# Two sequences' dispatch gathers as one step in the same four PSUM banks, in two of four sublayers of a two-layer macaron network

## The chip, the cores and the metric

The kernel runs on one core of a Trainium2 chip. A core has five engines with a queue each: TensorE (PE; its weight loads are listed as PEld) multiplies matrices into PSUM, VectorE (DVE) and ScalarE (ACT) read PSUM and SBUF, GpSimd (POOL) works in SBUF, and SyncE (SP) issues all DMA transfers here. The metric is device time in microseconds (us). The kernel before takes 718.74 us (median of three runs, 718.47 to 719.14).

## The reference, cut to what matters

The input is eight sequences of 256 tokens with 128 features, in float32.

```python
x = x + 0.5 * soft_moe(layernorm(x))       # 16 experts x 64 slots
x = x + linear_attention(layernorm(x))     # 16 heads, elu + 1
x = x + 0.5 * soft_moe(layernorm(x))
x = x + 0.5 * ternary_glu(layernorm(x))
x = x + favor_attention(layernorm(x))      # 16 heads, 32 random features
x = x + 0.5 * ternary_glu(layernorm(x))
# soft_moe, the part that the change touches (x normalized once more, se the slots' keys):
logits   = einsum('bnd,esd->bnes', x, se)          # 256 tokens x 1024 slots per sequence
dispatch = softmax(logits, axis=1)                 # over the tokens
combine  = softmax(logits over all slots)
slots    = einsum('bnd,bnes->besd', x, dispatch)   # "the gather": 1024 slots x 128 features
eout     = (gelu(slots @ Wg + bg) * (slots @ Wu + bu)) @ Wd + bd     # per expert
out      = einsum('bns,bso->bno', combine, eout)
```

## The kernel before, in words

The sequences are worked in two groups of four (G, BG). Both soft_moe sublayers of a group share one routine, so there are four such sublayers: (group 0, layer 0), (0, 1), (1, 0) and (1, 1). Between them run `linear` (after layer 0) and, after layer 1, `glu`, `favor` and `glu` again. The group's sublayer does `dispatch` for each of its four sequences, then `experts` once for the four together, then `combine` for each.

`dispatch(b)` normalizes the tokens, transposes them on TensorE (L455), and sends them out to DRAM and back (`replicated`, L637 to L652) so that a "k4" tile `yr` holds each 32-token block on its own quarter of the partitions. The logits (L670) are made with slots on partitions, 1024 slots as eight blocks of 128, and copied into a "comb" tile, from which the combine weights come later. A second "comb" tile `ex` takes the exponentials (L709), which GpSimd divides by their sums (L722) and VectorE transposes in blocks of 32 x 32 (L730), so that tokens stand on partitions. The gather (L743) then uses TensorE split into four groups of 32 rows: each group a multiplies its 32-token block with `ex` into a PSUM bank of its own, 256 columns wide, accumulating over the eight blocks c. Each PSUM bank holds 512 float32 values a partition; the gather fills half of each of four banks. Four evacuations (`affinely`, L557: ScalarE at L560 or VectorE at L562) scale and shift the banks into the "slots" tile `sl`. After that `dispatch` goes on to the maximum over slots (L758 to L790) and the exponentials of the combine weights (L796, L802).

`experts(sl)` fetches each expert's weights, 448 KB, into one of six "we" tiles (L823), multiplies the slots of all four sequences at once (L837), applies gelu on ScalarE (L843) and the product on VectorE (L848), multiplies back (L868), adds the bias (L874), and places the result over the slots by DMA (L881). `combine` (L910) multiplies the combine weights with it. The ternary layers' large products are L1124, their first and last ones L1193, L1196 and L1221; `favor` uses the column split (L1278, L1347, L1382: 32 columns of the array each) and the row split (L1297).

The order of all this is fixed in the file. Every piece of work is a `step`: the engines that may do it with an expected duration, what it reads and writes, and which tiles it takes. `ORDER` lists the steps' numbers; a negative number means the second of the two engines that a step allows (VectorE in place of ScalarE, GpSimd in place of VectorE). `Plan.place` goes through the list, gives each step the earliest time its engine, its inputs and a free tile allow, and picks the tile that has been free longest. It charges TensorE for a change between full array, row split and column split (`SPLIT`, L214) and ScalarE for a change of function table (`TABLE`). `Plan.issue` then writes out the instructions by planned start, each engine's in that order; where TensorE is planned to wait over 700 ns on a bank, it adds dummy matmuls (L1440). The tiles come in pools of fixed size (`kinds`, L327): nine "comb" of 8 KB a partition, four "k4" of 4 KB, eight PSUM banks "ps".

Of the kernel before, what the change touches and what calls it, by code (L numbers as in the profile page):

```python
# [16 lines left out]
    10, 11, 0, 37, 38, 3, 19, 20, 1, 2, 7, 8, 6, 4, 5, 13, 12, 40, 39, 41, 43, 53, 44, 42, 21, 22,  # L17
    23, 24, 14, 132, 133, -136, 172, 62, 63, 31, 134, 136, 137, 15, 16, 17, 18, 142, 140, 60, 9,
    143, 141, 32, 25, 26, -34, -35, 35, 36, 56, 1329, -28, 92, -29, 93, -96, -95, 98, 61, 173,
    1286, 1287, 148, -1290, 149, 29, -31, 68, 138, -1289, 146, 147, 57, 144, -146, 96, 97, 69,  # L20
    150, 66, 67, 64, 65, 163, 1292, 100, 73, -175, 104, 105, 70, 101, 102, 103, 106, 107, 164,
    139, -176, 176, 108, 1290, 177, 182, -1292, 180, 1294, 1330, -1332, -1333, 1333, 165, 166, 71,
    74, 178, 153, 109, 1334, 75, 76, 186, 187, 181, 184, 167, 72, 113, 114, 151, 183, 1345, 77,
    99, 154, 78, 82, 79, 80, 185, 81, 110, 1302, 1339, 51, 1295, 1337, 1338, 83, 115, 1342, 111,
    112, 116, 188, 155, 156, 117, 118, 193, 1335, 1336, 189, 1340, 152, 50, 1341, 190, 191, 194,
    119, 157, -123, 1343, 179, -121, 195, 1344, 1347, 121, 1346, 196, 192, 197, 158, 1299, 1348,
    160, 159, 162, 49, 161, 1349, 168, 48, 355, 203, 198, 200, -202, -200, 1372, 1296, 204, 1415,
    84, 85, 205, 202, 359, 366, 370, 1416, -1419, 1297, 1298, 1301, 1303, 360, 361, 356, 1304,
    357, 358, 1373, -1375, 250, 251, 252, 253, 1375, 1350, 1351, 254, 324, 325, 326, 1300, 328,
    334, 1353, 1376, 1377, 1310, 1305, 367, 379, 86, 368, 87, 88, 369, 206, -1418, 373, 338, 335,  # L30
    374, 219, 255, 256, 268, 90, 329, 371, 330, 372, 376, 327, 269, 1382, -208, 210, 341, 123,
    342, 1388, 339, 340, 336, 337, 1380, 1363, 1306, 1381, 170, 1384, 377, 220, 1307, 124, 125,
    -1390, 52, 345, 1385, 1354, 1355, 261, 223, 352, 353, 221, -1384, 224, 1387, 1378, 1356, 346,
    1386, 1320, 349, 350, 292, 293, 262, 225, 222, 347, 263, 1293, 1390, 1406, 236, 237, 296, 297,
    351, 1352, 265, 266, 281, 348, 264, 294, 1407, 1408, 240, 244, 1308, 241, 295, 242, 1409, 245,
    267, 47, 1357, 303, 298, 246, 304, 305, 306, 362, 363, 307, 308, 270, 1358, 243, 208, 209,
    1396, 310, 1421, 375, 1391, -1361, 378, 1311, 311, 278, 279, 1392, 1393, 1321, 1322, -1411,
    1411, 1312, 354, 257, 258, -1362, 1397, 271, 272, 1364, 273, 309, 274, 1365, 212, 213, 214,
    216, 275, 276, 229, 230, 231, 1398, 215, 233, 282, 1313, 286, 234, 235, 1362, 313, 217, 218,
    283, 317, 323, 1394, 1379, 232, 312, 287, 314, 1359, 364, 288, 238, 284, 277, 1419, 318, 319,  # L40
    285, 315, 316, 280, 1399, 1400, 1395, 259, 344, 1413, 1323, 1324, 169, 320, 321, 1420, 1366,
    343, 289, 290, 226, 227, 228, 91, -1368, 291, 1422, 126, 127, 130, 331, 131, 1309, 1412, 239,
    1370, 247, 1314, 248, 299, 1368, 332, 333, 1325, 260, 211, 1401, 1402, 171, 300, 1369, 249,
    1315, -1319, -1320, 301, 1316, 322, 1612, 1428, 1429, 1431, 1432, 89, 1538, -1404, 1439, 1423,
    1425, -1405, 1440, -1427, 1441, -1318, 365, 302, 1496, 459, 1424, 1434, 1427, 1435, 1436,
    1326, 381, 128, 45, 380, 382, 1442, 129, 1443, 433, 1437, 1528, 1438, 1327, 1430, 383, 384,
    432, 458, 434, 1517, 435, 1433, -386, 460, 461, 386, 1444, 1549, 1446, 436, 1448, 406, -1448,
    387, 1328, 388, -438, 407, 389, -439, 462, 463, 1405, 464, 1445, 1518, 408, 465, 1449, 439,
    1542, 1543, 1616, 1613, 1614, 409, 410, 412, 411, 1544, 1497, 1498, 1500, 1501, 1499, 1519,
    1520, 1539, 1540, 1617, 1521, 1529, 1550, 1551, 1553, 1541, 1615, 442, 1618, 440, 413, 1502,  # L50
    1514, 1530, 1554, 1555, 1552, 1515, 466, 1450, 1451, 1532, 1522, 1523, 441, 443, 445, 1452,
    1531, 391, 1533, 414, 1535, 416, 468, 1453, 1454, 1371, 1536, 467, 446, 1622, 1623, 444, 449,
    448, 469, 470, 1534, 1548, 1458, 474, 1456, 471, 472, 473, 1459, 392, 397, -397, 475, 1556,
    1566, 447, 393, 394, 395, 1507, 1567, 1537, 1511, 1512, 1513, 1508, 1509, 1510, 1460, 1461,
    1465, 1469, 1557, 390, 476, 477, 398, 1470, 1471, 46, 1466, 1467, 450, 415, 399, 417, 451,
    1468, 1601, 1414, 1569, 1591, 478, 400, 401, 1524, 1525, 479, 1545, 1546, 402, 419, 1462, 403,
    404, 405, 418, 422, 1568, 484, 485, 1475, 1516, 480, 420, 421, 1595, 423, 1596, 452, 453,
    1605, 1606, 1482, 1483, -488, 1547, 454, 1479, 1602, 486, 1597, -456, 1463, 1486, 1607, 1490,
    1558, 1464, 1603, -482, 456, 1604, 488, 457, 570, 571, 1487, 1488, 489, 573, 1472, 1473, 1476,
    1477, 482, 1478, 1625, 483, 613, 614, 1580, 1584, 1585, 1491, 54, 55, 1492, 492, 494, -494,  # L60
    496, 1506, -616, 497, -499, 495, 500, 501, -617, 617, 618, 424, 425, 1592, 426, 1581, 1611,
    1480, 1489, 499, -573, 1503, 1481, 1593, 1594, 502, 1582, 1583, 1457, 508, 574, 1608, 621,
    509, 626, 1609, 622, -576, 578, 1455, 427, 623, 503, 1504, 619, 629, 624, 518, 1559, 1563,
    510, -580, 1586, 1570, 1474, 490, 625, 491, 627, 628, 631, 632, 504, 505, 1527, 580, 1610,
    582, 583, 584, 511, 512, 1598, 1624, 1599, 1493, 1494, 1495, 519, 520, 630, 581, 1564, 1560,
    1561, 1562, 428, 1565, 506, 507, 1571, 1572, 429, 1619, 1620, 1485, 1574, 1575, 1576, 1577,
    430, 431, 527, 528, 1505, 1621, 633, 513, 1578, 1573, 1587, 529, 530, 531, 532, 637, 634, 635,
    638, 1484, -516, 1588, 589, 586, 537, -588, 585, 588, 535, 594, 540, 543, -545, 536, 541, 539,
    542, 514, 1579, 636, 1590, 1600, 1526, 1589, 1653, 639, 1652, 640, 521, 620, 576, 577, 1678,
    538, 546, 545, 551, 595, 596, 641, 1679, 597, 590, 591, 592, 552, 1680, 1654, 1655, 1656,  # L70
    -1658, 598, 1627, 553, 1626, 1628, 522, 547, 533, 548, -517, 517, 642, 644, 646, 593, 599,
    -1659, 643, 1659, -646, 549, 550, 554, 561, 555, 600, 534, 556, 559, 1629, 604, 558, 1660,
    -604, 1630, -1632, 1632, 557, 1662, 1705, 1633, 1681, 1682, -1685, 1704, 1706, 562, 563, 602,
    1707, 1708, 673, 799, -1684, 560, 601, 677, 678, 679, 1634, 674, 675, 803, 804, 805, 647, 800,
    810, 778, 782, 1661, -1710, 1710, 1711, 779, 1714, 726, 801, 802, 780, 1685, 676, 811, 812,
    648, 649, 684, 783, 784, 814, 815, 1664, -1669, 1669, 816, 813, 1635, 691, 688, 689, 820, 692,
    1637, 1639, 1638, 1712, 1686, 525, 821, 690, 781, 685, 686, 687, 1663, 1665, 1713, 1642, 1643,
    789, 1715, 1717, 564, -566, 1687, 1640, 1641, 701, 702, 796, 1644, 817, 1645, 1646, 1666,
    1667, 566, 567, 730, 797, 1647, 58, 1689, 1691, 1648, 1649, 1716, 1721, -1721, 818, 568, 1690,
    757, 1695, 1718, 1719, 1670, 1671, 523, 1692, 656, 660, -1695, 657, 1693, 1636, 1722, 1723,  # L80
    1672, 1673, 661, 727, 1724, 1725, 1688, 1650, 728, 729, 736, 1651, 790, 731, 732, 761, 650,
    651, 1696, 662, 1726, 1730, 743, 744, 762, 763, 1727, 663, 667, 791, 693, 1728, 1729, 668,
    669, 605, 1674, 1675, 704, 1731, 1697, -1734, 606, 793, -1733, 1734, 664, 683, 658, -1736,
    1859, 1860, 822, 1676, -1863, 1698, 1677, 1773, 1774, 652, 794, 795, 1699, 1746, 659, 792,
    1747, 1738, 1740, 1739, 1742, 1743, 1745, 665, 806, 705, 709, 1748, 703, 809, 666, 1700, 1701,
    807, 710, 737, 1744, 1754, 819, 607, 1741, 1749, 1702, 1703, 608, -1777, 738, 758, 759, 760,
    -1776, 706, -1862, 1865, 1863, -1865, 707, 740, 739, 680, 711, 681, 1869, 708, 741, 775, 776,
    654, 1867, 1750, 798, 1868, 768, 823, -1871, 1878, 1751, 1777, 569, 1779, 1875, 670, 671,
# [220 lines left out]
def macaron_kernel(ctx: ExitStack, tc: tile.TileContext, i: dict, out: bass.AP):  # L309


    nc = tc.nc
    B, N, D = out.shape
# [1211 lines left out]
```

## Time and profile before

| | |
|---|---|
| median of three runs | 718.74 us |
| the profiled execution | 720.09 us, of which the span from first to last instruction 718.4 us |
| TensorE busy | 710.3 us, 5266 matmul records |
| VectorE, ScalarE, GpSimd busy | 496.6, 391.4, 326.6 us |
| the gather (L743) | 1024 records, 59.5 us busy |
| its evacuations (L560, L562, "slots") | 42 and 22 instructions, 570 and 533 ns |
| granted TensorE clock | 1.00 |

The profile is one execution, recorded by the hardware. Float32 matmuls show as two records each, so 64 records of L743 are one sequence's gather (eight blocks times four row groups). A group's line gives the source line, engine and operation, the tiles written and read, the shapes, the number of instructions, then the engine's busy time, the mean duration, and the idle time just before them with the work that ended it. The chain that ended last is listed in order of time as start, length, engine, tile, line and records. Waits are "who <- released by whom: us in total, times, longest".

### The profile page before, as it was taken

The page shows a single profiled execution, that of the slowest core. Times are in us where ns is not written, and L with a number is a line of the kernel's source. Part 1 is how long each engine was busy: PE and PEld are TensorE (multiplying, and loading weights), DVE is VectorE, ACT ScalarE, POOL GpSimd, SP SyncE. Part 2 cuts the span into 40 slices and gives each one's busy share as a digit, 9 for nine tenths or more (in the row PEclk, how much of TensorE's full clock was granted, in tenths as well). Part 3 has the DMA queues.
Part 4 walks back from the last instruction along what each step waited for, and adds up shares of the span by engine and source line. Part 5 has one row for each costly group of instructions (what it writes and reads, how often), then busy time and mean ns, then how long its engine had stood idle before and what let it go on. Part 6 is the DMA issues. An engine that isn't in the chain of part 4 may idle for free.

```text
span 718.4 us, 14349 instructions
## 1 busy us (share of the span) xinstructions
PE 710.3 (99%) x5266; PEld 609.3 (85%) x5266; DVE 496.6 (69%) x1087; ACT 391.4 (54%) x780; POOL 326.6 (45%) x432
## 2 busy tenths in 40 slices
PE   8999999999999999999999999999999999999998
PEld 6889889998899999999788879876886878868787
DVE  7999774767997688974534545787576877875432
ACT  4987677464865547784642544566435542452421
POOL 6848377531327355745884321352425563413020
PEclk9999999999999999999999999999999999999999
DMA  4553566154344644462642321023404143241001
GB/s 134 162 201 99 165 160 225 34 157 124 118 113 134 182 133 127 120 195 90 203 137 67 84 67 43 18 61 89 73 16 89 44 92 58 59 90 30 12 11 37
DMA packets 118741, 72.76 MB, mean 101 GB/s; under 512 B 73360, under 2 KB 107536, under 8 KB 118672
## 3 DMA queue, kind: packets, MB, share of 16 engines
q1 hardware_dynamic: 118672, 71.85, 36.0%
q8 instruction: 42, 0.69, 0.4%
q14 instruction: 27, 0.22, 0.1%
HBM read 51.89 MB, written 11.53 MB: 88 GB/s over the span
## 4 chain that ended last, share of the span: by engine, by line
PE 95%; POOL 2%; DMA 1%; ACT 1%; DVE 1%; issue 0%; POOLq 0%; ACTq 0%
PE ps L1124 27%; PE ps L837 15%; PE ps L743 8%; PE ps L910 8%; PE ps L868 7%; PE ps L670 7%; PE ps L1221 4%; PE ps L1193 4%; PE ps L1196 4%; PE ps L455 2%; PE ps L1297 1%; PE ps L1347 1%; PE ps L1382 1%; PE ps L958 1%; DMA we<-in_We 1%; POOL sm L486 1%
## 5 line engine op out<-in xcount | busy, mean ns | idle before, releaser
L837 PE MATMUL ps<-slots,we 128*128 128x256 f32 x512 | 122.5, 380 | 1.8 <-ACT k L843 0.9
L837 PEld LDWEIGHTS ps<-slots,we 128*128 128x128 f32 x512 | 92.9, 190 | 14.8 <-ACT slots L560 1.2
L1124 PE MATMUL ps<-comb,comb 128*128 128x256 f32 x448 | 103.0, 380 | 0.0
L1124 PE MATMUL ps<-comb,slots 128*128 128x256 f32 x448 | 102.5, 380 | 0.0
L1124 PEld LDWEIGHTS ps<-comb,slots 128*128 128x128 f32 x448 | 84.1, 190 | 13.2 <-issue 1.8
L1124 PEld LDWEIGHTS ps<-comb,comb 128*128 128x128 f32 x448 | 83.6, 190 | 13.1 <-issue 1.7
L843 ACT ACTIVATE k<-ps,small 128x256 f32<-128x256 f32 x128 | 57.5, 475 | 60.1 <-PE ps L837 52.5
L796 POOL TENSOR_TENSOR comb<-comb,k 128x1024 f32<-128x1024 f32 x32 | 75.4, 2364 | 31.3 <-ACT k L460 8.8
L722 POOL TENSOR_TENSOR comb<-comb,sm 128x1024 f32<-128x1024 f32 x32 | 60.3, 1895 | 41.5 <-DVE sm L717 37.8
L848 DVE SCALAR_TENSOR_TENSOR k<-ps,small,k 128x256 f32<-128x256 f32 x128 | 57.4, 476 | 19.5 <-ACT k L843 18.2
L460 ACT COPY k<-ps 128x512 f32<-128x512 f32 (+2 forms) x52 | 25.6, 497 | 78.9 <-PE ps L1124 56.1
L868 PEld LDWEIGHTS ps<-we,k 128*128 128x128 f32 x512 | 63.6, 192 | 4.8 <-issue 2.0
L709 ACT ACTIVATE comb<-comb,sm 128x256 f32<-128x256 f32 x128 | 63.6, 507 | 4.6 <-DVE sm L701 2.4
L868 PE MATMUL ps<-we,k 128*128 128x128 f32 x512 | 65.7, 276 | 0.0
L484 POOL TENSOR_SCALAR sm<-sm 128x2 f32<-128x2 f32 x52 | 10.0, 193 | 121.7 <-DVE sm L478 112.1
L1138 DVE TENSOR_TENSOR comb<-ps,k 128x512 f32<-128x512 f32 x48 | 32.6, 686 | 47.1 <-PE ps L1124 35.3
L670 PE MATMUL ps<-k,seT 128*128 128x256 f32 x256 | 60.4, 383 | 0.8 <-ACT seT L596 0.4
L910 PEld LDWEIGHTS ps<-slots,comb 128*128 128x128 f32 x512 | 58.6, 192 | 1.3 <-issue 1.0
L910 PE MATMUL ps<-slots,comb 128*128 128x129 f32 x512 | 59.6, 276 | 0.0
L743 PE MATMUL ps<-comb,k 32*128 32x256 f32 x1024 | 59.5, 379 | 0.0
L1146 ACT ACTIVATE comb<-comb 128x512 f32<-128x512 f32 x48 | 29.3, 629 | 51.9 <-DVE comb L1138 51.8
L743 PEld LDWEIGHTS ps<-comb,k 32*128 32x128 f32 x1024 | 52.7, 185 | 4.5 <-ACT comb L460 0.3
(147 smaller groups left out, 1286.0 us busy)
## 6 DMA issues: line engine op xcount, KB each, us to landing
we<-in_We SPq DMA_DIRECT2D x64, 448.0 KB, 4.1
k<-y SPq DMA_DIRECT2D x64, 128.0 KB, 2.7
slots<-k SPq DMA_DIRECT2D x128, 64.0 KB, 2.1
t<-comb SPq DMA_DIRECT2D x8, 512.0 KB, 2.8
k<-t SPq DMA_DIRECT2D x32, 128.0 KB, 3.1
y<-k SPq DMA_DIRECT2D x16, 128.0 KB, 2.6
t<-k SPq DMA_DIRECT2D x16, 128.0 KB, 1.7
k<-t SPq DMA_DIRECT2D x64, 32.0 KB, 2.3
```

The lines of the kernel that those rows point to most:

```text
L670: mm(pl.ap[:, j, :], seT[:, 2 * u + j].rearrange("p k s -> p (k s)"), yt.ap, start=True, stop=True,)
L709: nc.scalar.activation(ex.ap[:, 4 * h + j, :], comb.ap[:, 4 * h + j, :], AF.Exp, bias=mx.ap[:, j : j + 1], accum_out=mx.ap[:, 4 + j : 5 + j],)
L722: return nc.gpsimd.tensor_tensor(ex.ap[:, part], ex.ap[:, part], mx.ap[:, 8:12].unsqueeze(2).to_broadcast([P, 4, N]), ALU.mult,)
L743: mm(po.ap, yr.ap[rows, TT * (c % 4) + c // 4, :], ex.ap[rows, :, 32 * c : 32 * c + 32], start=(c == 0), stop=(c == N // 32 - 1), tile_pos ...
L796: return nc.gpsimd.tensor_tensor(raw, raw, mb.ap.unsqueeze(1).to_broadcast([P, 4, N]), ALU.subtract)
L837: mm(pe.ap[:, m, :], we.ap[:, ts(2 * m + c, P)], sl.ap[:, j, k, :, 0:S], start=True, stop=True,)
L843: nc.scalar.activation(ga.ap, pe.ap[:, 0, :], AF.Gelu, bias=bg[:, e, c : c + 1])
L848: nc.vector.scalar_tensor_tensor(ht.ap[:, c, :], pe.ap[:, 1, :], bu[:, e, c : c + 1], ga.ap, ALU.add, ALU.mult,)
L868: mm(po.ap[:, r, :], ht.ap[:, c, ts(r, P)], we.ap[:, ts(4 + c, P)], start=(c == 0), stop=(c == 1),)
L910: mm(po.ap[:, t, 0 : D + 1], comb.ap[:, j, ts(t, P)], eo()[:, j, q, 0 : D + 1], start=(j == 0), stop=(j == NJ - 1),)
L1124: mm(bank.ap[:, o], w(k)[:, c, ts(o, P)], rhs().rearrange("p (c n) -> p c n", c=2)[:, c, :], start=(start and o + c == 0), stop=(stop and ...
L1138: nc.vector.tensor_tensor(C(i, k)(), bank.ap.rearrange("p o n -> p (o n)"), other(), ALU.add)
```

## The change

In the sublayers (0, 1) and (1, 0) the sequences are dispatched in pairs. `dispatch` ends where the gather began; a new function `gather` takes one or two sequences, allots four banks shaped (n, 8, 32), and issues first all matmuls of the first sequence into one half of the four banks and then those of the second into the other half, as one step. Each bank is then evacuated by one instruction for both sequences, 512 columns in place of 256. The maximum part of `dispatch` becomes a function `maxima`. In (0, 0) and (1, 1) a gather still holds one sequence. The "comb" pool has ten tiles and "k4" five; the scratch for dynamic DMA descriptors is set to 2048 bytes. There are 2506 steps in place of 2526, and `ORDER` is a new list throughout. `plan.tag` is a label that nothing in the file reads.

```diff
 ORDER = (
...
-        "comb": (NJ * N, 9),
+        "comb": (NJ * N, 10),
         "slots": (NJ * NB * 4 * S1, G),
-        "k4": (1024, 4),
+        "k4": (1024, 5),
...
-        pos = [ps_(NJ, 32) for _ in range(4)]
+        return comb, pm, ex, yr
+
+    def gather(b, got, sl):
+        plan.tag = (*plan.tag[:2], b)
+        n, q = len(got), b % BG
+        pos = [ps_(n, NJ, 32) for _ in range(4)]
 
         def gathered(_):
-            for c in range(N // 32):
-                for a, po in enumerate(pos):
-                    rows = slice(32 * a, 32 * a + 32)
-                    mm(
-                        po.ap, yr.ap[rows, TT * (c % 4) + c // 4, :], ex.ap[rows, :, 32 * c : 32 * c + 32],
-                        start=(c == 0), stop=(c == N // 32 - 1), tile_position=(32 * a, 0),
-                    )
-
-        step({"PE": 3455}, gathered, [yr, (ex, 0), (ex, 1)], pos, split=1)
...
+            for k, (_, _, ex, yr) in enumerate(got):
+                for c in range(N // 32):
+                    for a, po in enumerate(pos):
+                        rows = slice(32 * a, 32 * a + 32)
+                        mm(
+                            po.ap[:, k], yr.ap[rows, TT * (c % 4) + c // 4, :],
+                            ex.ap[rows, :, 32 * c : 32 * c + 32],
+                            start=(c == 0), stop=(c == N // 32 - 1), tile_position=(32 * a, 0),
+                        )
+
+        needs = [c for _, _, ex, yr in got for c in (yr, (ex, 0), (ex, 1))]
+        step({"PE": 3455 * n}, gathered, needs, pos, split=1)
         for a, po in enumerate(pos):
             affinely(
-                lambda a=a: sl.ap[:, :, a // 2, q, 32 * (a % 2) : 32 * (a % 2) + 32],
-                lambda po=po: po.ap, [po], [(sl, "in", q, a)], NJ * 32,
-            )
-
+                lambda a=a: sl.ap[
+                    :, :, a // 2, q : q + n, 32 * (a % 2) : 32 * (a % 2) + 32
+                ].rearrange("p j q s -> p q j s"),
+                lambda po=po: po.ap, [po], [(sl, "in", q + k, a) for k in range(n)], n * NJ * 32,
+            )
+
+    def maxima(b, comb, pm, late):
...
             sl = Buf("slots", (P, NJ, 2, BG, S1))
-            combs = {b: dispatch(b, sl, g + layer == 0) for b in bs_}
+            plan.tag = (g, layer)
+            first, single = g + layer == 0, g == layer
+            combs = {}
+            for b in bs_ if single else bs_[::2]:
+                got = [dispatch(b + k, sl, first) for k in range(1 if single else 2)]
+                gather(b, got, sl)
+                for k, (comb, pm, _, _) in enumerate(got):
+                    maxima(b + k, comb, pm, first)
+                    combs[b + k] = comb
...
-    nc = bacc.Bacc("TRN2", target_bir_lowering=False, num_devices=1)
+    nc = bacc.Bacc("TRN2", target_bir_lowering=False, num_devices=1, dynamic_dma_scratch_size=2048)
```

## The prediction

> **What bounds the kernel now.** I read the busy shares first, then the chain that ended last, then TensorE's own waits.
>
> ```profile
> PE 710.3 (99%) x5266; PEld 609.3 (85%) x5266; DVE 496.6 (69%) x1087; ACT 391.4 (54%) x780; POOL 326.6 (45%) x432
> ...
> PE 95%; POOL 2%; DMA 1%; ACT 1%; DVE 1%; issue 0%; POOLq 0%; ACTq 0%
> ```
>
> TensorE is both busiest and, for 95% of the span, the chain itself. Its granted clock is full in every slice. So an edit counts only where it removes work or a hole from TensorE's stream, or makes one. The chain in order of time prices both (start, length, line, records):
>
> ```profile
> 30.11 3.85 PE ps L743 x64
> 33.96 3.65 PE ps L670 x16
> 37.61 3.67 PE ps L743 x64
> 41.28 1.09 PE ps L1440 x8
> 42.37 4.12 PE ps L743 x64
> ...
> 106.08 7.12 PE ps L743 x128
> 113.19 3.65 PE ps L670 x16
> ...
> 309.59 3.46 PE ps L670 x16
> ...
> 381.95 3.46 PE ps L1124 x16
> ...
> 521.11 1.86 PE ps L1382 x32
> ...
> 562.70 1.00 PE ps L1382 x16
> 563.70 3.65 PE ps L1124 x16
> ```
>
> L743 is the gather, 64 records a sequence. A gather alone takes 3.67 us, two behind each other 7.12, so the second costs 3.45 and entering the four-row-group split costs 0.22. L670, full-array work, takes 3.65 right after a gather and 3.46 elsewhere: leaving costs 0.19. The column split (L1382) costs 0.14 to enter (1.00 alone; 1.86 for two, so 0.86 each) and 0.19 to leave (L1124, 3.65 against 3.46). The 380 ns that the groups show for a 256-column record is its latency; what it occupies is the 216 ns of 3.46/16.
>
> TensorE's waits, over 150 ns, are few:
>
> ```profile
> PE ps L837 <- ACT k L843: 0.9, 1, 0.9
> PE ps L837 <- DMA we<-in_We: 0.6, 1, 0.6
> PE ps L455 <- DVE k L493: 0.5, 1, 0.5
> ```
>
> I then summed TensorE's steps in written order at the spacing of these rows (0.216 us a 256-column record, 0.1115 a 128-column one, 0.43 a 512-column one, 3.455 a gather, and the switches): 697.7 us. From the first flip at 6.57 to the last matmul's end, 709.90 + 5.37 = 715.27, there are 708.7. So about 11.0 us are holes and dummy matmuls. Laid against the chain's times they lie so: 5.6 us up to 33.96 (the start: keys, norms, first logits), 1.75 between 41.28 and 46.49 (the dummy row, with a second switch on each side of it), 1.5 up to 113, 1.7 up to 204, 1.0 up to 309, nothing after that. Call that sum's running total the work clock.
>
> **The change part by part.**
>
> *Gathers in pairs.* Matmuls, shapes and columns are the same: no work goes. What goes is switching. Counted off the two orders: before, TensorE's list goes from full to row split 11 times, row to full 18, full to column 14, column to row 7, column to full 7; after, 9, 16, 13, 7 and 6. (The row split also serves a step of the last attention sublayer.) The old order already runs the eight gathers of the two sublayers in five runs (the rows of 64 to 191 records between 82 and 232 us), the new one their four pairs in three: two runs go, and one column run besides. Sum: 2 x 0.22 + 2 x 0.19 + 0.14 + 0.19 = 1.15 us, on the chain: -1.15.
>
> *Evacuations.* 32 instructions of 128x256 become 16 of 128x512.
>
> ```profile
> L560 ACT ACTIVATE slots<-ps,small 128x256 f32<-128x256 f32 x42 | 21.9, 570 | 20.1 <-PE ps L743 20.1
> ```
>
> VectorE's twin (L562) has 533 ns. A 512-column one is estimated from the copies of L460 and L462 (373 to 589 ns on ScalarE, 415 to 689 on VectorE): 0.79 and 0.81 us. 32 x 0.55 - 16 x 0.80 = 4.8 us leave two engines at 54% and 69%: nothing on the chain. If their cover went, the most they could give is those 4.8.
>
> *The finished half waits.* The first sequence's half of a bank is read 3.45 us later than today. Nobody waits for it: the experts (L837) read all four sequences of a group, and ScalarE already idles 20.1 us before these evacuations. The Trainium skill (PSUM — Partial Sum Buffer, "Summary: rules for kernel authors") says to read PSUM during matmuls only from another bank, which speaks against sharing one. By that rule alone each paired sublayer's last half is held 3.45 us longer, 6.9 us in all; by the row above it is 0, since the other half is the later one anyway.
>
> *What is late next: the cover after the last gather.* On the work clock, before: group 0's second sublayer has 4.0 us between the last gather and its first expert (combine work), after: 1.98. Needed: 0.15 from matmul to reader (three gathers from 220.44 with 0.22 of entry and a 0.24 wait end at 231.27; the reader starts at 231.42), two evacuations on each engine, 1.6, and 0.15 back to TensorE: 1.9. It just fits: cost 0, and up to 1 us if either engine comes 1 us late. The other paired sublayer goes from 3.8 to 7.3.
>
> *The extra tiles.* One "comb" and one "k4" more make room where a pair holds two sequences' exponentials and replicated tokens; the order may use them anywhere. Their space comes out of the descriptor scratch: 71.85 MB go over the hardware queue, 0.69 and 0.22 over the two instruction queues, none over a software one, so the smaller scratch costs 0 (bounds: 0 both ways, as no transfer shown uses it). `plan.tag` issues nothing.
>
> *The new order.* Everything moves. ScalarE's table loads go from 57 to 64, counted off the exp/gelu/silu sequence: 7 x 1.28 = 9.0 us more on an engine at 54%, with ACT waiting 52.5 us on L837 and 56.1 on L1124 as cover; without it up to 9.0 would show. GpSimd takes 4 more norm applications (460 ns) and 2 more subtractions (1.28 us), 4.4 us at 45% busy; VectorE loses as many. SP issues as many transfers, but in another sequence (below). At the start the keys' norm comes ahead of the tokens'; the first logits need both, so 0. Chains inside TensorE's list keep room: the shortest distance from an expert's second hidden step to its down step falls from 1.97 to 1.73 us, against about 1.5 needed (0.2 + 0.475 ScalarE + 0.15 + 0.476 VectorE + 0.15).
>
> What the order does to the holes no row shows. Bounds: all 6.0 us after 33.96 vanish (the 400 us after 309 show that an order can run without any) or the rate of 46.49 to 204, 3.2 us in 158, doubles, +3.2. I take the value nearest to today's, because the opening and the mix of steps are alike, less half of the 1.7 us lost between 113 and 204: there the linear sublayer's first step now stands 14 us earlier on the work clock (117.4 against 131.1), which loosens its chain of small steps. -0.85.
>
> Sum: -1.15 - 0.85 = -2.0 us. The profiled execution (span 718.4, 720.09 with what lies around it) would give 718.1; it stands 1.35 above the median of 718.74, which goes to 716.7.
>
> **The rivals.**
>
> *Switches only, the rest a wash.* The holes stay or grow by up to 2.5: 717.6 if they stay. For it: the opening lists of both orders are nearly equal, and 5.6 of 11.0 us lie there. Against: half of the rest lies where the order changed. Under this the change reads as no change.
>
> *Weights come late (slower).* On SP, before, six weight fetches left at 115.1 to 118.8, 16 us before group 1's first expert at 135.00. After, all six stand behind the second pair's spreads and behind the turned squares of sequence 0, which need its combine. Counted from that combine's end: update and norm 0.8 + 0.9 + 1.1 + 0.9, transpose 0.4, spill 0.3 + 1.7, place 2.6 make 8.7, and the first fetch lands 0.45 + 4.1 later, at 13.3; the first expert is due at 18.0, the fifth at 23.2, the sixth at 25.8.
>
> ```profile
> we<-in_We SPq DMA_DIRECT2D x64, 448.0 KB, 4.1
> ```
>
> At 225 GB/s, the busiest slice, a fetch takes 2.0 us and the sixth lands at 23.3: in time. At 136 GB/s, the mean from 200 to 235 us, 3.3 us: the sixth lands at 29.8, 4.0 late, net +2.85: 721.6. It decides from about 3.0 us a fetch. Against it: only 0.6 us of TensorE's waits fell to a fetch.
>
> *Nearly all holes close.* -1.15 - 5.0: 712.6. For it: two pools are larger. Against: the waits named are spread over ScalarE, VectorE and transfers.
>
> *The pair's cover fails.* The 1.98 us are missed by 2, and the pair's first gather waits 1 for its partner: net +1.85, 720.6.
>
> **How the numbers follow.** Forecast 0.45; switches only 0.26; late weights 0.11; all holes 0.12; cover fails 0.06. A measurement tells about 0.2%, 1.44 us, from no change: forecast and closed holes are faster (0.57), the wash is same (0.26), the others slower (0.17). The likeliest case by itself spans 715.5 to 717.3. Leaving out half of the closed-holes case below and most of the late weights above gives 713.4 to 720.8.
>
> **What would show it.** Right: the chain shows the gathers of group 1's first sublayer as two rows of 128 records near 7.1 us and those of group 0's second as one of 256 near 14.0, L560 and L562 split into 256- and 512-element forms, TensorE's work unchanged, and its holes between 34 and 309 us at 5 us or less. Wrong: a wait of L837 on a weight fetch near 125 us, or on L560 or L562 near 225, of 1 us or more; holes summing to over 7; gathers that take other than 3.45 us each; ScalarE, with its seven added table loads, named as releaser of TensorE.

## The result and the profile after

The changed kernel takes 720.72 us (median of 11 runs, 719.64 to 721.74) against 719.13 us before (11 runs, 717.71 to 719.83). The ratio is 1.0028, with a 95% interval of 1.002 to 1.0036: slower by a quarter of a per cent, where 2 us less were forecast. The profiled execution of after has a span of 718.0 us and took 719.73 us, near the low end of its own runs. That of before (720.09) lies above every one of these 11 runs of before. The two traces alone would therefore say "no change"; the runs say slower.

First the busy shares and the chain that ended last, from the page of after, and the evacuations by form:

```profile
PE 709.7 (99%) x5264; PEld 610.6 (85%) x5264; DVE 496.3 (69%) x1083; ACT 392.6 (55%) x769; POOL 330.2 (46%) x438
...
PE 90%; POOL 3%; DVE 2%; DMA 2%; ACT 2%; issue 1%; SPq 1%; POOLq 0%; ACTq 0%; DVEq 0%
...
we<-in_We SPq DMA_DIRECT2D x64, 448.0 KB, 4.3
```

```profile
L558 ACT ACTIVATE slots<-ps,small 128x256 f32<-128x256 f32 x22 | 11.0, 567 | 15.3 <-PE ps L750 15.1
...
L558 ACT ACTIVATE slots<-ps,small 128x512 f32<-128x512 f32 x9 | 6.7, 778 | 25.4 <-PE ps L750 25.4
L560 DVE TENSOR_SCALAR slots<-ps,small 128x512 f32<-128x512 f32 x7 | 5.5, 803 | 5.1 <-PE ps L750 5.1
```

TensorE's share of the chain fell from 95% to 90%, and SP's queue (SPq), which was not on the chain before, has 1% of it. The longer evacuations cost 778 and 803 ns, close to the 0.79 and 0.81 us estimated. Line numbers have moved: the gather is L750, the experts' first product L848, the logits L671.

The chain in order of time (start, length, line, records):

```profile
86.97 3.41 DMA slots<-k
91.31 1.96 PE ps L848 x8
...
101.64 7.12 PE ps L750 x128
...
122.90 7.12 PE ps L750 x128
...
158.18 2.42 DMA k<-t
...
220.43 14.03 PE ps L750 x256
...
273.18 1.97 DMA y<-k
...
276.67 2.06 DMA k<-y
```

The gathers stand as forecast: two rows of 128 records at 7.12 us and one of 256 at 14.03. But transfers are now on the chain at 87, at 158 and from 273 to 279 us, where the chain of before had, behind its start, one weight fetch at 166.86. TensorE's waits name new places:

```profile
PE ps L848 <- DVE k L885: 1.0, 1, 1.0
...
PE ps L991 <- DMA k<-t: 0.4, 1, 0.4
```

The most useful measure here is one that the page doesn't print. `Plan.place` has given every step a planned start, switches included. The lag is a TensorE step's start in the trace less that planned start. It shows where a kernel loses time against its own intention, whatever its order. The planned ends are 715.88 us before and 714.62 after, so the plan itself grants the change 1.27 us, 1.16 of it switches and the rest a little less planned waiting. Lag in us at a planned time:

| kernel | 60 | 80 | 100 | 170 | 245 | 310 | end |
|---|---|---|---|---|---|---|---|
| before | -0.28 | -0.15 | 1.00 | 2.07 | 2.52 | 2.54 | 0.33 |
| before, second trace | -0.30 | -0.17 | 0.32 | 1.10 | 1.53 | 1.54 | -0.68 |
| after | 0.72 | 0.95 | 2.40 | 2.94 | 2.85 | 3.31 | 1.23 |
| after, second trace | 0.77 | 1.00 | 2.37 | 3.62 | 3.66 | 3.97 | 1.89 |

(After 310 us all kernels run ahead of the plan, by 1.8 to 2.2 us up to the end.) At 60 us, ahead of any paired gather, after lies 1.0 us further behind its plan than before does, and both kernels then lose 1.8 to 3.2 us between 60 and 310.

### The profile page after: what moved, and what is told of

Same layout as the page of the kernel before. It is cut to its first block, busy times and chain, and to the rows that moved or that the text cites. A ratio compares the mean times of both kernels' runs of the same rounds, so it can differ in the third digit from the quotient of the medians.

```text
span 718.0 us, 14325 instructions
## 1 busy us (share of the span) xinstructions
PE 709.7 (99%) x5264; PEld 610.6 (85%) x5264; DVE 496.3 (69%) x1083; ACT 392.6 (55%) x769; POOL 330.2 (46%) x438
## 4 chain that ended last, share of the span: by engine, by line
PE 90%; POOL 3%; DVE 2%; DMA 2%; ACT 2%; issue 1%; SPq 1%; POOLq 0%; ACTq 0%; DVEq 0%
PE ps L1137 27%; PE ps L848 13%; PE ps L750 8%; PE ps L922 8%; PE ps L879 7%; PE ps L671 5%; PE ps L1235 4%; PE ps L1207 4%; PE ps L1210 4%; PE ps L453 2%; PE ps L1312 1%; PE ps L1397 1%; PE ps L1362 1%; PE ps L970 1%; POOL sm L484 1%; POOL comb L723 1%
## 5 line engine op out<-in xcount | busy, mean ns | idle before, releaser
L848 PE MATMUL ps<-slots,we 128*128 128x256 f32 x512 | 122.4, 381 | 1.1 <-DVE k L885 1.0
L848 PEld LDWEIGHTS ps<-slots,we 128*128 128x128 f32 x512 | 93.3, 190 | 15.6 <-issue 2.0
L671 PE MATMUL ps<-k,seT 128*128 128x256 f32 x256 | 62.1, 382 | 0.7 <-ACT seT L594 0.4
L750 PE MATMUL ps<-comb,k 32*128 32x256 f32 x1024 | 58.7, 378 | 0.2 <-DVE sm L718 0.2
L1122 POOL TENSOR_TENSOR comb<-comb 128x512 f32<-128x512 f32 x23 | 29.3, 1272 | 59.7 <-DVE comb L1216 25.9
L750 PEld LDWEIGHTS ps<-comb,k 32*128 32x128 f32 x1024 | 52.6, 185 | 4.3 <-DVE sm L718 0.6
```

Source lines behind the costliest of these rows:

```text
L671: mm(pl.ap[:, j, :], seT[:, 2 * u + j].rearrange("p k s -> p (k s)"), yt.ap, start=True, stop=True,)
L750: mm(po.ap[:, k], yr.ap[rows, TT * (c % 4) + c // 4, :], ex.ap[rows, :, 32 * c : 32 * c + 32], start=(c == 0), stop=(c == N // 32 - 1), ti ...
L848: mm(pe.ap[:, m, :], we.ap[:, ts(2 * m + c, P)], sl.ap[:, j, k, :, 0:S], start=True, stop=True,)
```

## The experiments

Three theories. T: transfers come late, because the new order leaves less room on SP's queue ahead of TensorE. P: the pairs themselves cost something. S: the extra tiles or the smaller descriptor scratch cost something. All ratios are to runs of before that were taken beside the kernel in question.

### The two kernels again

> The kernel before, unchanged, as a second look. Both theories: 719.1 us, within 0.7 of it. Theory T (transfers come late): TensorE's holes after 46 us that end with a DMA or with work just behind one sum to under 2 us, and differ from the first profile by up to 1 us. Theory P (the pairs themselves cost): nothing is said of this one.

> The changed kernel, unchanged, as a second look. Both theories: 720.7 us, +0.28% on the kernel before. T: against the written plan it falls behind by 1 to 3 us more than in the first profile, and does so at steps fed by a transfer (weights, expert outputs, turned squares), not at the pairs. P: it falls behind by 1.5 us or more at the three runs of paired gathers and at the first expert after each.

No edit. Before 718.75 us (ratio 1.0001, 0.9992 to 1.001), after 720.76 us (1.0028, 1.0016 to 1.0041). The second traces hold the key. After, second trace, the chain:

```profile
88.63 5.40 DMA we<-in_We
...
131.36 7.22 DMA we<-in_We
138.63 6.31 PE ps L848 x28
```

This time two weight fetches are on the chain by name. The one issued at 131.36, the second of six, needs 7.22 us to land, and the second expert of group 1's first sublayer starts 0.05 us after it (the first had started at 137.08 without a wait).

In the first trace of after, the wait at 91.31 was put down to VectorE (L885). Here are VectorE and TensorE at that place, first in this first trace, then in the second one (start, length, and in brackets the idle time before and its releaser):

```profile
90.84 0.41 DVE L885 TENSOR_TENSOR k<-ps,we 128x256 f32<-128x256 f32 x1
...
91.31 1.96 PE L848 MATMUL ps<-slots,we 128*128 128x256 f32 x8 [0.97 <-DVE k L885]
```

```profile
90.93 0.41 DVE L885 TENSOR_TENSOR k<-ps,we 128x256 f32<-128x256 f32 x1
...
90.81 1.97 PE L848 MATMUL ps<-slots,we 128*128 128x256 f32 x8 [0.39 <-DMA we<-in_We]
```

It is the same program, and in the second trace TensorE's step starts 0.12 us before that VectorE instruction begins. So it can't need it. The releaser named was merely the last thing to end before the start. What the step needed was its weights: the landing of each fetch, the last signal of its semaphore, is in the trace too. Expert 0's fetch landed at 91.17 in the first trace and at 90.67 in the second, 0.14 us ahead of the step both times.

The same holds for before, and this undoes a piece of the prediction's evidence. Its longest wait (0.9 us, "L837 <- ACT k L843") against the same place in the second trace of before:

```profile
97.36 0.49 ACT L843 ACTIVATE k<-ps,small 128x256 f32<-128x256 f32 x1
...
97.88 1.96 PE L837 MATMUL ps<-slots,we 128*128 128x256 f32 x8 [0.86 <-ACT k L843]
```

```profile
97.34 0.49 ACT L843 ACTIVATE k<-ps,small 128x256 f32<-128x256 f32 x1
...
97.19 1.97 PE L837 MATMUL ps<-slots,we 128*128 128x256 f32 x8 [0.21 <-DMA we<-in_We]
```

Again the second trace starts L837 before that ScalarE instruction begins, and names the fetch (landed at 97.74 in the first trace, 97.06 in the second). So that wait too did not belong to ScalarE.

The same can be done for all 64 fetches of a kernel. The next table sums what the lag grows by at those first uses that start less than 0.2 us after their fetch landed, and names the larger ones (start, growth, both in us). The last column is the growth at the linear sublayer's step at 161 us (L991 in after), which needs turned squares, the transfer `k<-t`.

| kernel | at fetches | where | at L991 |
|---|---|---|---|
| before | 2.24 | 97.88: 1.02, 157.18: 0.51, 171.94: 0.72 | none |
| before, second trace | 1.30 | 97.19: 0.36, 156.11: 0.12, 170.97: 0.81 | none |
| after | 1.50 | 91.31: 1.13, 94.38: 0.16, 138.12: 0.12 | 0.53 |
| after, second trace | 1.81 | 90.81: 0.55, 94.17: 0.44, 138.63: 0.67 | 0.75 |

So transfers make most of the lag that both kernels gain from 60 us on, and weights cost before as much as after: 1.77 and 1.66 us in the mean of two traces. What after has on top is the wait for the squares. In its plan they land 0.05 us before their use. Neither theory's full forecast came: the second trace of after lost 0.6 us more from 60 to 310 than the first, where T had said 1 to 3, and across the paired gathers and the steps up to the first expert the lag moves by less than 0.25 us in the first trace, where P had said 1.5.

One of these losses does come from pairing, by way of the plan. `fetch` is a step that reads the cell that the third sequence's first evacuation writes; with pairs, the evacuation of the whole pair writes it. In group 1's first sublayer that cell is ready at 109.51 us by the plan of before, and the six fetches are planned from 113.14 on, with 9.5 to 18.3 us of room. In after it is ready at 128.67 and they are planned from 128.72 on, with 0.9 to 2.3 us. That is the place of the 0.12 and 0.67 us. The losses at 91 to 94 us lie in group 0's first sublayer, where nothing is paired.

### The tiles alone

```diff
-        "comb": (NJ * N, 9),
+        "comb": (NJ * N, 10),
-        "k4": (1024, 4),
+        "k4": (1024, 5),
-    nc = bacc.Bacc("TRN2", target_bir_lowering=False, num_devices=1)
+    nc = bacc.Bacc("TRN2", target_bir_lowering=False, num_devices=1, dynamic_dma_scratch_size=2048)
```

> The kernel before, its order untouched, with ten comb and five k4 tiles and the small descriptor scratch; each engine's list is the same, only which tile a step takes differs. T and P: 719.1, ratio 1.000 +- 0.001. A third theory, S (more tiles or the smaller scratch slow transfers or engines): 720.7, ratio 1.002 or more.

719.26 us, ratio 1.0011 (1.0002 to 1.002). Against the 718.6 us of before beside it that is 0.7 us, a small loss of its own that may reach 0.2%. The profiled span, 717.5 us, lies between the two of before, and its lag at 310 us is 1.70, between before's 1.54 and 2.54, so no place of the loss is shown. S can carry a part of the result, not the whole: `after_sp` below has the same tiles and scratch and is faster than before.

### No dummy matmuls in the gathers

```diff
-            if s.idle > 700:
+            if s.idle > 700 and s.start < 12000:
```

> The changed kernel without the seven dummy matmuls that stand behind 12 us (three ahead of the second gather, four ahead of the third, where the split is left and entered again for them). T and P: 0.2 to 0.4 us less than the changed kernel, 720.4, if the clock holds; if TensorE's granted clock falls in the holes of 1 us that stay, up to 1 us more, 721.5. The rest of the difference to the kernel before stays under every theory.

721.03 us, ratio 1.0032 (1.0022 to 1.0041), clock 1.00 throughout. That is not the 0.2 to 0.4 us less that was expected, and not told apart from after (1.0016 to 1.0041). Ahead of the second gather, which starts at 37.90 in both, a wait stands in place of three dummies:

```profile
PE ps L750 <- ACT comb L458: 0.6, 1, 0.6
```

The third gather, without its four, starts 1.04 us earlier (41.89 against 42.93), but its last record starts at 46.30 against 46.29: its first records stand further apart. So the dummy rows only fill waits. They cost nothing that is seen here, and without them nothing is won.

### SP's list alone, in the changed kernel

ORDER is rewritten so that the lists of TensorE, VectorE, ScalarE and GpSimd stay as they are in after, and 186 of the 257 places in SP's list change. The stretch that matters first, with planned issue times in us (fetch: an expert's weights; place: an expert's result over the slots; yspread: a sequence's tokens, replicated, for group 1's gathers; load0: a constant):

```diff
-... fetch 5 @80.5  place 3 @81.0  yspread 5 @82.4  fetch 0 @84.2  place 12 @84.7  fetch 6 @87.7  yspread 4 @88.2
+yspread 5 @28.4 ... yspread 4 @56.3 ... fetch 5 @80.5  load0 @81.0  place 3 @81.4  fetch 0 @82.8  fetch 6 @87.7
```

> The changed kernel with only SyncE's list rewritten (186 of its 257 places; the lists of TensorE, ScalarE, VectorE and GpSimd are word for word those of the changed kernel): transfers go out earlier where the written plan leaves them room, its end unchanged. T (transfers come late): 0.8 to 1.6 us less than the changed kernel, about 719.5. P (the pairs cost by themselves): as the changed kernel, 720.7.

717.54 us (717.25 to 717.85, 11 runs), ratio 0.9982 (0.9974 to 0.9991): 3.2 us less than after (before took 718.91 beside this one and 718.6 beside that one) and 1.4 us less than before. SP's queue at this place, after and then `after_sp` (start, time in the queue):

```profile
81.41 0.33 SPq L834 DMA_DIRECT2D we<-in_We  x1
81.84 1.64 SPq L892 DMA_DIRECT2D slots<-k  x2
83.58 2.87 SPq L644 DMA_DIRECT2D k<-y  x4
86.55 0.38 SPq L834 DMA_DIRECT2D we<-in_We  x1
```

```profile
82.54 1.24 SPq L888 DMA_DIRECT2D slots<-k  x2
83.88 5.08 SPq L830 DMA_DIRECT2D we<-in_We  x2
```

In after the fetch of expert 0 stands behind a spread of four transfers, which are first read at 101.64, by group 1's first gathers. The spread was planned to start at 82.4 us and started at 83.58, and its four issues held the queue for 2.87 us, so the fetch left at 86.55 where 84.2 was planned, and landed at 91.17. In `after_sp` it is the first of the last row's two fetches: it leaves at 83.88 and lands at 87.73 (the row's length is mostly the wait of the second, which leaves at 88.63). TensorE's step that uses it starts at 91.31 and 90.22, the second without a wait. The Trainium skill (Perfetto Trace Analysis, "Per-instruction lifecycle: what the profiler-reported window actually captures") says that for a DMA the whole movement of data lies outside the window that the profiler reports. The rows agree: the fetch of expert 0 shows 0.38 us in after and landed 4.62 us after its issue; the median of all 64 is 4.3.

With SP's list rewritten no wait on a transfer is left among TensorE's waits, no first use of a fetch starts within 0.2 us of its landing, and the chain is TensorE's again:

```profile
PE 94%; POOL 2%; DVE 1%; DMA 1%; ACT 1%; issue 0%; SPq 0%; POOLq 0%; DVEq 0%
```

```profile
PE ps L1462 <- POOL ident masks.py:199: 1.6, 1, 1.6
PE ps L667 <- ACT seT L590: 0.6, 2, 0.4
PE ps L667 <- ACT k L554: 0.4, 1, 0.4
PE ps L449 <- POOL k L487: 0.3, 1, 0.3
PE ps L966 <- DVE k L456: 0.3, 1, 0.3
PE ps L746 <- DVE sm L714: 0.2, 1, 0.2
```

Its lag is 0.72 us at 60, 1.01 at 100, 0.66 at 170, 0.57 at 245, 0.86 at 310: flat from 60 on, where after gained 2.6 to 3.2. The pairs, the evacuations and the table loads are all still in it, and across the paired gathers and the steps up to the first expert its lag moves by less than 0.25 us. T had said 0.8 to 1.6 us and P none; it was twice as much. So rewriting SP's list is worth the 3.2 us, and the pairs by themselves hold none of them. The edit has one thing beside it: the new list also changes which tile of its pool 1298 of the 2506 steps take. TensorE's planned starts are the same to the step.

This does not make late transfers the whole reason why after is slower than before. Before has waits of the same kind, and no run rewrites its SP list alone for more room.

### Late fetches alone, in the kernel before

Nothing paired, and all other engines' lists as before. Only weight fetches change places in SP's list (76 of 257 places differ; 20 fetches leave later by plan, by up to 18 us, 18 earlier), so that the plan's end stays but more of them land just in time: 13 of 64 within 0.5 us of their use by plan, where before has 5. For example:

```diff
-fetch 15 @113.1  fetch 8 @113.6  fetch 4 @114.1  fetch 7 @115.0  fetch 6 @115.5  fetch 9 @116.0  sqspill @132.2
+fetch 15 @109.5  fetch 6 @114.0  fetch 7 @114.9  fetch 8 @115.4  sqspill @132.2  fetch 4 @132.5  fetch 9 @133.0
```

> The kernel before with only weight fetches moved to later places in SyncE's list (76 of 257 places differ), as late as its written plan allows at the cost of 0.1 us; all compute lists untouched, no pairs. T: 0.8 to 2.0 us more than before, 719.5 to 720.7, with TensorE's waits on weights over 1 us. P: as before, 718.7.

720.14 us, ratio 1.002 (1.0011 to 1.0029). Fetches with less room and nearly the same plan (715.98 us) cost 1.2 us, with no pair in the kernel; here too the list changes the tiles of some steps (895). Its waits name other engines (L833, the experts' first product, on ACT 0.8 us and on DVE 0.7 us), but the two steps start at 97.78 and 172.20, 0.14 and 0.13 us after their fetch landed. In all 2.33 us of its lag stand at fetches, little more than the 2.24 and 1.30 of before, so the trace doesn't show where the 1.2 us went; the edit is what shows them.

### Orders with room for longer transfers, without and with pairs

If T is the whole matter, an order that leaves room should gain for both kernels, and the pairs' switches should then show. Each kernel's whole ORDER was searched anew so that its planned end moves little when transfers take longer. The third column is `Plan.place` run over the same list with every transfer landing 0.6 us later:

| kernel | planned end | planned end, transfers 0.6 us longer | fetches of 64 that land within 0.5 us of their use, by plan | median measured |
|---|---|---|---|---|
| before | 715.88 | 724.6 | 5 | 718.75 |
| after | 714.62 | 726.6 | 10 | 720.76 |
| before_late | 715.98 | 729.2 | 13 | 720.14 |
| after_sp | 714.62 | 721.8 | 6 | 717.54 |
| before_spare | 715.70 | 716.5 | 0 | 716.62 |
| after_spare | 714.48 | 715.1 | 0 | 717.01 |

The diff of each searched kernel is the list alone, 2465 of 2526 and 2432 of 2506 entries.

> The kernel before, no pairs, nine and four tiles, with an order searched anew so that the plan holds its end (715.7 in place of 715.9) also if every transfer lasts 0.3 to 1.2 us longer. T: 1 to 2 us less than before, 717.2. P: as before, 718.7, at best 718.5.

> The changed kernel, pairs and all, with an order searched in the same way for the same time (planned end 714.5, 1.2 less than the kernel before searched so). T: 1.2 us less than that one, about 716.0, since the saved switches then reach the end. P: at least 1 us more than that one, 718 or over.

Without pairs 716.62 us, ratio 0.9972 (0.996 to 0.9983); with pairs 717.01 us, 0.9974 (0.9963 to 0.9985). An order searched for room gains 2 us without any pair. All lists are new in it, so the edit alone doesn't single out SP's queue. But the kernel with pairs, 1.2 us better by plan, came out 0.4 us behind; T had said about 716.0, P 718 or over, and neither came. So either the pairs cost, or something else in the searched order with pairs does. The lag tells where to look: at 60 us, ahead of any paired gather, it is -0.39 without and +0.40 with pairs in the kernel, and at 310 us the paired one stands at 0.47.

### The opening

Both kernels once more beside each other, and a third: `after_spare` with the 190 steps or so of the first 45 us in the order that `before_spare` has. 186 list entries differ. They hold no paired gather, but 30 of those steps prepare two sequences that a pair gathers later (their norms and logits).

> The same kernel as before_spare (no pairs, an order searched so that longer transfers do not move the planned end), taken again beside the next two. T (transfers that come late) expects 716.4 to 717.0 again, TensorE no later against the written plan at 60 us than -0.3.

> The same kernel as after_spare (pairs, an order searched in the same way), taken again. T expects 716.8 to 717.2 again. P (the pairs themselves cost) expects it slower than before_spare2 by more than its interval although its plan is 1.2 us shorter.

> after_spare with the steps of the first 45 us in the order in which before_spare has them; no pair is dispatched there, and the rest of the list is unchanged. Planned end 714.55, as after_spare. If the 0.7 us by which every order with pairs was behind its plan at 60 us come from those opening lists, TensorE stands near -0.3 there and the time falls to 716.0 to 716.4, below before_spare2 by 0.3 to 0.8. P expects no change against after_spare2.

716.74 us (716.63 to 716.85), 717.01 (716.98 to 717.05) and 716.49 us (716.45 to 716.82); ratios 0.9971 (0.9958 to 0.9983), 0.9974 (0.9963 to 0.9985) and 0.9967 (0.9954 to 0.9979). As P had said, the kernel with pairs is slower than the one without, by 0.3 us, and their runs don't overlap, though the intervals of the ratios do; but exchanging the opening takes that away. The opening alone is worth 0.5 us. The chain of `after_spare2`, then of `after_spare_open`:

```profile
42.11 1.09 PE ps L1463 x8
43.20 3.73 PE ps L747 x64
46.93 1.06 PE ps L668 x4
47.99 3.67 PE ps L747 x64
51.66 0.37 PE ps L450 x2
```

```profile
41.56 0.71 PE ps L1463 x4
42.27 4.07 PE ps L747 x64
46.34 1.06 PE ps L668 x4
47.40 3.67 PE ps L747 x64
51.06 0.37 PE ps L450 x2
```

The third gather of group 0 starts 0.93 us earlier behind a shorter dummy row, and the stream is 0.6 us earlier afterwards. Its lag at 60 us is -0.24, as expected, and the time just misses the 716.0 to 716.4 us that were. In the three traces no lag is gained at a fetch.

The part with pairs is not closed. `after_spare_open` is the fastest kernel run, but its lead over `before_spare2`, 0.25 us, lies within the spread of their runs, where the plans differ by 1.15 us. Its lag ends at -1.95 against -2.87, so 0.9 us go missing. Behind 60 us, steps of the lag of over 0.12 us sum to 1.28 us in it (at 180, 280, 306 and from 416 to 418 us; experts, logits and the ternary layer) and to 0.62 in `before_spare2` (at 81, 328 and 523). None of them is at a paired gather. What causes them was not tried.

## Why the prediction was wrong, point by point

**Bound.** That TensorE's stream sets the end, and that an edit counts only by what it does to that stream's work, switches and holes, held where it can be tested: `after_sp` has TensorE's work and switches of after, and its 3.2 us came with holes closed.

**Switches, -1.15.** Confirmed as work: the written orders have 1.16 us less of it by the plan's prices, and the rows of 7.12 and 14.03 us show the gathers without the switch between. That it reaches the end of a kernel isn't shown: of 1.15 us by plan between `before_spare2` and `after_spare_open`, 0.25 came.

**Evacuations and the cover after the last gather: 0.** Right. After the row of four gathers, the next expert starts on TensorE without a wait (chain, from 230 us):

```profile
229.92 4.53 PE ps L750 x84
234.45 0.58 PE ps L453 x4
235.04 0.45 PE ps L999 x4
235.48 0.45 PE ps L991 x4
235.93 0.43 PE ps L995 x2
236.37 3.53 PE ps L848 x16
```

From 234.46 to 236.37 are 1.91 us of cover, and ScalarE and VectorE end their two evacuations at 235.94 and 236.10.

**The finished half waits: 0.** Right for TensorE at the gathers, but "nobody waits for it" was wrong: by the plan the weight fetches of the sublayer wait for the third sequence's evacuation, and in group 1's first sublayer that moved all six behind the pair. It cost 0.1 and 0.7 us there. The prediction's estimate of 6.9 us by the Trainium skill's page (PSUM — Partial Sum Buffer, "Summary: rules for kernel authors") did not come; across the paired gathers of `after_sp` the lag moves by less than 0.25 us. (The rule's second choice, another quadrant of the same bank, was not open here: each evacuation reads 128 partitions.)

**Tiles and scratch: 0.** Measured alone at 1.0011 (1.0002 to 1.002), 0.7 us, and not located.

**Table loads and GpSimd's added work: 0.** Right: `after_sp` has all of them and its lag is flat.

**The holes from 34 us on: -0.85.** This is the step that failed. TensorE's holes can be counted as the time between two of its steps less the planned lengths of the steps between (on this count before has less than the prediction's 6.0 us):

| holes, us | 34 to 60 | 60 to 309 |
|---|---|---|
| before, two traces | 1.56, 1.56 | 2.84, 1.86 |
| after, two traces | 2.76, 2.79 | 2.73, 3.33 |
| after_sp | 2.80 | 0.14 |

They did not shrink by 0.85 but grew by 1.9 in the mean: 1.2 between 34 and 60 us and 0.7 behind. For the first part the prediction took the value nearest to before's, on the ground that the openings are alike. It had looked at the keys' norm, ahead of 34 us; the lists differ further on, and the new plan itself has two rows of dummy matmuls there, ahead of the second and the third gather, where the old one has one. Exchanging the opening lists gave 0.5 us back in `after_spare`. What in them does it was not tried.

For the second part it took half of the 1.7 us lost between 113 and 204 as won, since the linear sublayer's chain of small steps stands looser. In before those losses are not in that chain: 0.51 and 0.72 us stand at experts whose weights had just landed (0.12 and 0.81 in the second trace). And in after that chain has a wait that it hadn't, 0.53 and 0.75 us for its turned squares. What the term missed was the nature of these holes: they are transfers, and rewriting SP's list removes them. The room of transfers on SP's queue (10 fetches within 0.5 us of their use against 5, the squares 0.05 us) was never counted. The parts of the holes that the prediction lists also sum to 11.55 us, not to its total of 11.0.

**What is left open.** The two traces of each kernel differ by 0.5 us in their means (720.07 against 719.58), about what the holes and switches give (1.9 less 1.16). The medians differ by 1.6 and 2.2 us: the profiled executions of before were long ones, those of after short ones. So some 1 us or more of the slowdown is in no trace. The tiles' 0.7 us may be part of it.

**The rival "weights come late", 0.11.** Its 721.6 us lie near the 720.7 measured, but by luck. It had one fetch, the sixth of group 1's first sublayer, 4.0 us late at 3.3 us a fetch. There the six fetches left between 130.71 and 135.41 as described and landed about 1.7 us apart (134.71 to 143.34), and the sixth cost nothing; the second cost 0.1 and 0.7 us. The larger loss, 1.3 and 1.0 us at the fetches from 91 to 94 us, lies in group 0's first sublayer, where the prediction had not followed SP's queue; and before loses as much at its own. The argument against it, that only 0.6 us of TensorE's waits fell to a fetch, was wrong: 2.24 us of lag did in that trace.

**What would show it.** The gathers, the forms and the unchanged work came as listed under "right"; the holes did not (5.5 and 6.1 us by the count above, where before has 4.4 and 3.4). The list under "wrong" named a wait of L837 on a fetch near 125 us of 1 us or more. The nearest are 0.7 us at 138 in one trace, and 1.0 us at 91 under another engine's name.

## What to carry to other kernels

When a hand-written order is replaced, walk the DMA queue's list as carefully as TensorE's: for each fetch, what stands ahead of it on the queue, how long those issues hold it, and how much room the plan leaves from landing to first use. A plan whose end grows by 9 to 13 us when every transfer takes 0.6 us longer, as those of before, after and before_late do, has no room for what these traces show, and the orders searched for longer transfers were the faster ones here. (It ranks them only roughly: before_late grows more than after and is faster.) And a wait's named releaser is the last thing that ended, no more: compare it with the landing of the step's transfers, and with a second trace of the same program, before an argument rests on it. Last, when a change joins two pieces of work, look for every step that was allowed to start after the first of them.

## What the runs showed of the hardware

- Four issues of one spread held SP's queue for 1.97 us in one trace and 2.87 us in another at the same place, and the two placements ahead of them for 2.29 and 1.64. The fetch behind left at 86.36 and 86.55 where 84.2 was planned.
- A weight fetch of 448 KB landed 4.3 us after its issue in the median. Of six in a row, issued between 130.71 and 134.44, the first took 3.99 us, the second 7.22 and the last 8.90.
- A matmul that waited for its weights started 0.13 to 0.14 us after the fetch had landed at ten of the twelve places that the table of the fetches names, and 0.05 us after it at the other two.
- Kernels whose orders leave room for transfers are also steadier: their runs lay within 0.07 to 0.37 us in the last set, those of before within 1.6 us, those of after within 2.1. One run of `before_spare` in the set ahead of it, 717.70 against 716.62, stands apart; its trace has a fetch that cost 0.38 us.
- Without the dummy matmuls, with a wait of 0.6 us in place of a row, the granted clock stayed at 1.00.
